# A clear, four selections and twelve subtractions put elsewhere in a gated cross-attention kernel with routed experts

## The chip, the cores and the metric

The kernel runs on one core of a Trainium2 chip. A core has five engines with queues of their own: TensorE (PE, with its weight loads shown as PEld), VectorE (DVE), ScalarE (ACT), GpSimd (POOL) and SyncE (SP). Each works through its instructions in order, and they meet through semaphores. TensorE writes its products to PSUM, which has eight banks of 128 x 512 float32 here; VectorE and ScalarE read them out, GpSimd works on SBUF alone. The metric is the device time of one execution in microseconds (us), lower is better.

## The reference

Four sequences of 512 tokens with 256 features pass through two layers. Each layer adds a gated cross-attention to a context of 512 tokens (16 heads of 16 features) and a gated feed-forward block. Reduced to what matters:

```python
x = x + tanh(g_xattn[0]) * L0_xattn(layernorm(x), ctx)   # with a bias by distance in time
x = x + tanh(g_ffn[0])   * L0_ffn(layernorm(x))          # weights rounded to -1, 0, 1; 256 -> 1024 -> 256
x = x + tanh(g_xattn[1]) * L1_xattn(layernorm(x), ctx)
x = x + tanh(g_ffn[1])   * L1_ffn(layernorm(x))

def L1_xattn(q, k, v):                                   # queries, keys and values after a relu
    E = NORM * einsum('bqhd,bkhd->bhqk', qh, kh)
    return einsum('bhqk,bkhd->bqhd', softmax(E, axis=-1), vh)

def L1_ffn(x):                                           # 2048 tokens, 4 experts, the best one of each token
    expert = argmax(x @ W_router, axis=-1)
    h = gelu(einsum('th,ehi->tei', x, W1) + b1, approximate=False)
    y = einsum('te,tei->ti', one_hot(expert, 4), h) @ Wo + bo + x
    return layer_norm(y) * ln_gamma + ln_beta
```

## The kernel before

**Attention.** Work is cut into 32 groups (layer, sequence, half of the heads' tiles, even or odd heads), in that order, and each group into four units, 128 in all. Per unit, `scores` (L535) issues two kinds of products: those whose rows give each query's maximum (`maxima`, L500; VectorE reduces them, L512), six units ahead, and those that give the weights (`weights`, L516; ScalarE takes the exponential, L527; in layer 0 GpSimd multiplies a block by the decay, L530). The maximum is subtracted ahead of time, inside the query: after the last maxima of a group, `shifted` (L563) turns them with four TensorE transposes into one PSUM bank (pmT) and VectorE subtracts this bank from the queries (L571). `slot` (L1199) places that call in the third unit of the group before, so the next group's first weights stand two units later. `weighted` (L548) multiplies with the values, `divided` (L600) turns the sums and divides, and in layer 1 adds them to x (L623, GpSimd mostly).

All other work (projections, layer norms, the first feed-forward block, routing) is a list of steps with a cost and a due unit, and `slot` puts them between units in program order. So every engine's order is fixed when the program is built.

**Routing.** `route` (L709) normalizes a sequence, writes rows to DRAM, and ranks each token within its expert. `dispatch` (L781) makes lists of tokens per tile of 128, four lists in all. For list i: `lists` and `token_places` (many small VectorE operations), `by_tile` (L950: a one-hot of tile and token, `tid`, in a cleared space of 128 x 512), `picked` (L983: four selections `sel` of 128 x 512 at L986 for 16 token blocks), `collected` (L994: TensorE products `pidT` of tid and sel, read out by ScalarE), `tokens` (L1006: the token numbers, which later row fetches need). The fourth list (i = 3) is of three mixed tiles, each of two experts.

**Experts.** After the attention 16 tiles (TT) go through `turn_tile` (t: transposes ptx, L1065), `hidden_half` (h: products pg, L1090, and ScalarE's Gelu, L1116; tiles from 13 on have two experts and 64 products) and `output_tile` (o: products pyf, L1285). `sum_tile` (L1293), `norm_tile` (L1308) and `put_tile` (L1321) follow each o on VectorE, with a root on GpSimd (L1304) and an indirect store from GpSimd's queue. `fetch_rows` (L1030) and `fetch_weights` (L1047) are indirect DMAs from that queue too. The queue of items is written by hand (L1359); around the change it is t9, o8, t10, h9, h10, t11, o9, h11. What `dispatch` does in this part hangs on the items in the table `steps` (L1351), and each item's steps stand after its products and fetches and before its sums and norm:

```python
        ("h", 8): [mixes[2]], ("o", 7): [mixed_places], ("o", 8): [mixed_tiles],
        ("h", 9): mixed_sels, ("h", 10): [mixed_collected], ("o", 9): [mixed_tokens],
...
        if kind == "o":
            sum_tile(j)
        if kind == "o" and 0 < j < TT - 2:
            norm_tile(j - 1)
```

Here `mixed_tiles` is the fourth list's `by_tile`, `mixed_sels` its four `picked`. So VectorE has at o8: by_tile of the fourth list, sums of tile 8, norm of tile 7; then, at h9, the four selections. GpSimd has at o8: rows and weights of tile 12, the clear of tid (L959), the root of tile 8, the store of tile 6.

Of the kernel before, what the change touches and what calls it, by code (L numbers as in the profile page):

```python
# [11 lines left out]
F32 = mybir.dt.float32  # L12
U32 = mybir.dt.uint32
AF = mybir.ActivationFunctionType
ALU = mybir.AluOpType
# [4 lines left out]
P = 128  # L20
B, S, D = 4, 512, 256
# [30 lines left out]
def flamingo_kernel(ctx: ExitStack, tc: tile.TileContext, t: dict, out: bass.AP):  # L52
    nc = tc.nc
# [4 lines left out]
    const = ctx.enter_context(tc.tile_pool(name="const", bufs=1))  # L58
# [5 lines left out]
    def bank_psum(name):  # L64
        return ps.tile([P, 512], F32, tag="bank", name=name)
# [37 lines left out]
    wo0 = const.tile([P, NC, D], F32, tag="wo0", name="wo0")  # L103
# [288 lines left out]
    xTs, qs, ks, q2s, pos, os_ = {}, {}, {}, {}, {}, {}  # L392
# [170 lines left out]
    def shifted(s):  # L563

        g = groups[s]
        m = m_sb[g[0]][g[3]]
        pm = bank_psum(f"pmT{s}")
        for n in range(NT):
            nc.tensor.transpose(pm[:, ts(n, P)], m[:, n].rearrange("p h w -> p (h w)"), ident)
        q2s[g] = act.tile([P, S], F32, tag="q2", name=f"q2_{s}")  # L570
        nc.vector.tensor_tensor(q2s[g], qs[g], pm, ALU.subtract)  # L571

# [206 lines left out]
    def dispatch(i):  # L781
# [3 lines left out]
        behind = i > 1  # L785
# [3 lines left out]
        def small(shape, tag):  # L789
            return sml.tile([P, *shape], F32, tag=f"d_{tag}", name=f"{tag}_{nm}", bufs=1)  # L790

        def across(v, *shape):
            return v.to_broadcast([P, *shape])
# [4 lines left out]
        def space(name):  # L798
            if i == 1:

                if not spaces:
                    two = act.tile([P, 2, S], F32, tag="xT", name=f"{name}_{nm}", bufs=2)
                    spaces.extend(two[:, k] for k in (1, 0))
                return spaces.pop()
            if behind:
                return act.tile([P, S], F32, tag="sel", name=f"{name}_{nm}", bufs=5)
            return wts.tile([P, S], F32, tag="xg", name=f"{name}_{nm}", bufs=4)
# [142 lines left out]
        def by_tile():  # L950

            place1 = st["place1"]
            ge = small([TT, T_LIST + 1], "ge")[:, 0:K, 0 : T + 1]
            nc.vector.tensor_tensor(
                ge, across(place1.unsqueeze(2), K, T + 1),
                across(made["tiles_of"][:, 0 : T + 1].unsqueeze(1), K, T + 1), ALU.is_gt,
            )
            tid = space("tid").rearrange("p (k w) -> p k w", w=HP)
            nc.gpsimd.memset(tid, 0.0)  # L959
            st["tid"] = tid  # L960
            tid = tid[:, 0:K, 0:T]
            nc.vector.tensor_tensor(tid, ge[:, :, 0:T], ge[:, :, 1 : T + 1], ALU.subtract)
            nc.vector.tensor_tensor(tid, tid, across(made["token"][:, 0:K].unsqueeze(2), K, T), ALU.mult)
            row1 = small([TT], "row1")[:, 0:K]
            nc.vector.tensor_reduce(row1, ge[:, :, 1 : T + 1], AX.X, ALU.add)
            nc.vector.scalar_tensor_tensor(row1, row1, float(-P), place1, ALU.mult, ALU.add)
            st.update(row1=row1)
# [48 lines left out]
        if j0 == T_ONE:  # L1016
            return (
                [fewest_and_most(m) for m in range(T_MIX)], mixed_places, by_tile,
                [picked(k) for k in range(0, K, 4)], collected, tokens,
            )  # L1020
        return [
            (lists, 0, 0), (token_places, 0, 0), (by_tile, 0, 1),
            *((picked(k), 0, int(k == 0)) for k in range(0, K, 4)),
            (by_expert, 0, 0), (collected, 0.15 * LISTS[i][0] + 0.3, 1), (tokens, 0.3, 1),
# [174 lines left out]
    def slot(u):  # L1199
# [4 lines left out]
        if u % NT == 2 and u > 0:  # L1204
            s = u // NT
            if s + 1 < len(groups):
                shifted(s + 1)
                used += 0.5
            if s > 0 and not by_blocks(s - 1):
                divided(s - 1)  # L1210
                used += 0.5
# [38 lines left out]
    for u in range(-NT, n_units):  # L1250
        if u == 0:
            shifted(0)
            early_values()
            other_constants()
        if u == 4:
            maxima_places(1)
        if u == first_unit(0, B - 1) + 1:
            attn_w.append(load_attn(1))
        if u == first_unit(1, 2) + 2:

            wo1 = [const.tile([P, NF // 2, D], F32, tag=f"cT{i}", name=f"wo1{i}") for i in range(2)]
            for i, w in enumerate(wo1):
                rw = t["wo1"][i * FF // 2 : (i + 1) * FF // 2, :]
                nc.sync.dma_start(out=w, in_=rw.rearrange("(c p) f -> p c f", p=P))
        vs = [u + NT] if u < 0 else [2 * u + NT, 2 * u + NT + 1] if u < LEAD - NT else [u + LEAD]
        scores(u, [v for v in vs if v < n_units])
        if u < -NT + 2:
            values[u + NT][0]()
        if u == -NT + 1:
            early_rows()  # L1270
        if u == -1:
            keys[0](halves=[1])
        if u in totals:
            job, i = totals[u]
            job(i)
        slot(u)
# [55 lines left out]
    for f2 in range(2):  # L1332
# [15 lines left out]
    mixes, mixed_places, mixed_tiles, mixed_sels, mixed_collected, mixed_tokens = dispatch(3)  # L1348
# [3 lines left out]
        ("o", 1): [turn3], ("o", 2): [products3], ("o", 3): [logits3],  # L1352
        ("h", 5): [ranks3, lists, token_places, by_tile], ("o", 4): [*sels, by_expert],
        ("o", 5): [collected], ("h", 7): [tokens, mixes[0]], ("o", 6): [mixes[1]],
        ("h", 8): [mixes[2]], ("o", 7): [mixed_places], ("o", 8): [mixed_tiles],
        ("h", 9): mixed_sels, ("h", 10): [mixed_collected], ("o", 9): [mixed_tokens],
    }
    first = LISTS[2][1]
    queue = [("h", 4), ("o", 0), ("o", 1), ("o", 2), ("t", 5), ("o", 3), ("h", 5)]  # L1359
# [130 lines left out]
```

## Time and profile before

| | |
|---|---|
| time, median of 3 runs | 844.43 us (844.37 to 845.02) |
| time of the profiled execution | 841.69 us |
| its span | 839.6 us |
| TensorE busy | 809.5 us, 96% |
| VectorE busy | 568.7 us, 68% |
| ScalarE busy | 422.1 us, 50% |
| GpSimd busy | 270.3 us, 32% |

The times of the profile are those of one execution, and stand against its own 841.69 us. The page has 40 slices of 21 us each; a digit is the busy share of a slice in tenths, and PEclk is the clock that TensorE was granted. A line of the groups names the source line, the engine, what is written and read, the count, busy time and mean duration, and then the idle time just before, with what ended it. A line of the timeline has start and duration in us. In the chain of waits each line is what ended last, in order of time: start, duration, what. A busy TensorE is not TensorE at its peak: where the banks come free late, its products start apart from each other.

The groups of instructions that the change touches or that stand nearest to it:

```profile
L530 POOL TENSOR_TENSOR p<-p,dec 128x256 f32<-128x256 f32 x128 | 93.6, 735 | 177.1 <-ACT p L527 177.1
L561 ACT COPY oT<-po 128x512 f32<-128x512 f32 x32 | 18.7, 584 | 77.1 <-PE po L555 77.1
L571 DVE TENSOR_TENSOR q<-q,pmT 128x512 f32<-128x512 f32 x32 | 21.7, 677 | 1.1 <-PE pmT L569 1.1
```

### The profile page before, as it was taken

Reading aid. Unit: us, or ns where it says so; the run is one execution under the profiler, and the core shown is the slowest. Engines: PE = TensorE matmul, PEld = TensorE weight load, DVE = VectorE, ACT = ScalarE, POOL = GpSimd, SP = SyncE. Lnnn points to the kernel's source line nnn. Section 1 sums busy time; section 2 is a strip of 40 time slices with the busy share of each in tenths; the row PEclk is TensorE's granted clock in tenths of the full one; section 3 lists DMA queues with packets and bytes.
Section 4 is the critical chain, followed back from the end, with each engine's and each line's share of the span. In section 5 each row is a group of like instructions: output and inputs, shape, how many; then the busy total and the mean of one; then the engine's idle time right before and its main releaser. Section 6 shows DMA issues by size and latency. Waiting matters only on the chain. (4 is left out here: it accounts for less than half of the span.)

```text
span 839.6 us, 13573 instructions
## 1 busy us (share of the span) xinstructions
PE 809.5 (96%) x5220; PEld 452.3 (54%) x5220; DVE 568.7 (68%) x1272; ACT 422.1 (50%) x884; POOL 270.3 (32%) x439
## 2 busy tenths in 40 slices
PE   6999999999999999999999999999999999997995
PEld 3444344535464345544474444554445546896994
DVE  6868868766857676567746777448688663886443
ACT  2575555653645453455526475336655667332341
POOL 5636445524233253321101030002103422544522
PEclk9999999999999999999999999999999999998998
DMA  9200000000001000000000000000104331736620
GB/s 313 72 1 1 1 1 1 1 1 1 1 1 39 1 1 1 1 27 1 1 1 26 1 24 28 1 1 1 52 1 152 126 106 59 284 119 218 241 78 31
DMA packets 17712, 42.27 MB, mean 50 GB/s; under 512 B 2033, under 2 KB 12017, under 8 KB 15217
## 3 DMA queue, kind: packets, MB, share of 16 engines
q0 software_dynamic: 5104, 27.34, 9.3%
q1 hardware_dynamic: 12128, 13.54, 4.8%
q8 instruction: 41, 0.67, 0.3%
q10 hardware_dynamic: 416, 0.54, 0.2%
q14 instruction: 23, 0.18, 0.1%
HBM read 35.13 MB, written 6.29 MB: 49 GB/s over the span
## 5 line engine op out<-in xcount | busy, mean ns | idle before, releaser
L512 DVE TENSOR_REDUCE m<-pm 128x1 f32<-128x512 f32 x512 | 316.8, 682 | 107.2 <-PE psc L498 104.8
L527 ACT ACTIVATE p<-psc 128x512 f32<-128x512 f32 x512 | 267.1, 602 | 151.4 <-PE psc L498 148.9
L498 PE MATMUL psc<-q,k 32*128 32x512 f32 x1024 | 278.3, 622 | 0.2 <-DVE h L676 0.2
L498 PE MATMUL pm<-k,q 32*128 32x512 f32 x1024 | 262.2, 615 | 1.5 <-ACT q L485 0.9
L530 POOL TENSOR_TENSOR p<-p,dec 128x256 f32<-128x256 f32 x128 | 93.6, 735 | 177.1 <-ACT p L527 177.1
L498 PEld LDWEIGHTS pm<-k,q 32*128 32x128 f32 x1024 | 92.7, 184 | 83.8 <-issue 49.8
L498 PEld LDWEIGHTS psc<-q,k 32*128 32x128 f32 x1024 | 106.2, 183 | 51.6 <-issue 25.5
L555 PE MATMUL po<-p,v 128*32 128x512 f32 x1024 | 116.5, 595 | 1.9 <-DVE m L512 1.9
L555 PEld LDWEIGHTS po<-p,v 128*32 128x32 f32 x1024 | 31.7, 109 | 81.8 <-issue 60.8
L1090 PE MATMUL pg<-xs,wg 128*128 128x128 f32 x608 | 71.6, 276 | 0.4 <-DVE m L512 0.4
L1090 PEld LDWEIGHTS pg<-xs,wg 128*128 128x128 f32 x608 | 69.8, 192 | 3.8 <-DVE m L512 1.4
L623 POOL TENSOR_TENSOR x<-x,o 128x256 f32<-128x256 f32 x14 | 10.2, 728 | 174.4 <-DVE o L616 131.7
L1116 ACT ACTIVATE ha<-pg,wg 128x128 f32<-128x128 f32 x120 | 34.2, 368 | 53.6 <-PE pg L1090 53.6
L668 PE MATMUL ph<-xTf,w1q 128*128 128x512 f32 x128 | 60.0, 605 | 0.0
L1285 PE MATMUL pyf<-wo,ha 128*128 128x256 f32 x256 | 58.6, 384 | 0.0
L561 ACT COPY oT<-po 128x512 f32<-128x512 f32 x32 | 18.7, 584 | 77.1 <-PE po L555 77.1
L383 PE MATMUL py_f<-w2q,h 128*128 128x256 f32 x256 | 57.2, 381 | 0.0
L383 PEld LDWEIGHTS py_f<-w2q,h 128*128 128x128 f32 x256 | 48.0, 190 | 9.4 <-DVE m L512 3.0
L1285 PEld LDWEIGHTS pyf<-wo,ha 128*128 128x128 f32 x256 | 48.4, 194 | 6.2
L455 PE MATMUL pk<-cT,wk 128*128 128x512 f32 x68 | 35.3, 644 | 7.2 <-DMA cT<-in_ctxT_dram 7.2
L668 PEld LDWEIGHTS ph<-xTf,w1q 128*128 128x128 f32 x128 | 22.6, 189 | 30.4 <-issue 18.2
L388 DVE SCALAR_TENSOR_TENSOR x<-py_f,tg,x 128x512 f32<-128x512 f32 x8 | 6.0, 751 | 42.8 <-PE py_f L383 42.8
(256 smaller groups left out, 814.6 us busy)
## 6 DMA issues: line engine op xcount, KB each, us to landing
x<-in_x_dram SPq DMA_DIRECT2D x4, 512.0 KB, 8.8
rows_d<-xn_f SPq DMA_DIRECT2D x4, 512.0 KB, 3.0
rows_d<-x SPq DMA_DIRECT2D x4, 512.0 KB, 3.6
cT<-in_ctxT_dram SPq DMA_DIRECT2D x3, 512.0 KB, 9.6
w1q<-in_w_dram SPq DMA_DIRECT2D x1, 1024.0 KB, 8.9
w2q<-in_w_dram SPq DMA_DIRECT2D x1, 1024.0 KB, 11.2
wo<-in_wo_dram SPq DMA_DIRECT2D x2, 512.0 KB, 3.8
rows<-in_rows_dram SPq DMA_DIRECT2D x1, 640.0 KB, 9.1
```

The lines of the kernel that those rows point to most:

```text
L383: nc.tensor.matmul(py[:, n, :], lhsT=operand(c, n0 + n), rhs=w[:, c, :], start=(c == 0), stop=(c == chunks - 1),)
L455: nc.tensor.matmul(pp, lhsT=attn_w[layer][w][:, c, ts(tt, P)], rhs=src[:, c, :], start=(c == 0), stop=(c == NC - 1),)
L498: nc.tensor.matmul(out_, lhsT=lhs[r, ts(n, P)], rhs=rhs[r, :], start=True, stop=True)
L512: nc.vector.tensor_reduce(m[:, n, 2 * pair + i, r : r + 1], pm[i], AX.X, ALU.max)
L527: nc.scalar.activation(p[:, i, :], psc[i], AF.Exp, scale=SCALE)
L530: nc.gpsimd.tensor_tensor(d, d, dec.unsqueeze(1).to_broadcast([P, 2, P]), ALU.mult)
L555: nc.tensor.matmul(po[i * HP : (i + 1) * HP, :], lhsT=v_sb[b % 2][0][:, kt, c0 : c0 + HP], rhs=ps_exp[NT * s + kt, i // 2][:, i % 2, :], s ...
L561: nc.scalar.copy(pos[s], po)
L668: nc.tensor.matmul(ph, lhsT=w1q[:, c, ts(f, P)], rhs=st["xT"][:, c, :], start=(c == 0), stop=(c == NC - 1),)
L1090: nc.tensor.matmul(ph[:, f, :], lhsT=w[:, c, ts(f2 * NF // 2 + f, P)], rhs=xs[j][:, c, :], start=(c == 0), stop=(c == NC - 1),)
L1116: nc.scalar.activation(ha[:, f, :], (ha if src is None else src)[:, f, :], AF.Gelu, bias=biases[j][:, fa : fa + 1],)
L1285: nc.tensor.matmul(py, lhsT=hs[j, f // 4][:, f % 4, :], rhs=wo1[f // 4][:, f % 4, :], start=(f == 0), stop=(f == NF - 1),)
```

## The change

Three edits. In `shifted`, for the second layer's sequences 1 to 3 (twelve groups), ScalarE copies the bank of turned maxima into SBUF, in the place that the first layer's output weights had, and GpSimd subtracts it from the queries; the other twenty groups stay with VectorE. In `by_tile`, the clear of `tid` is VectorE's for the two lists made after the attention (`behind`), and GpSimd's for the others as before. In `steps`, the fourth list's selections move from h9 to o8, behind its `by_tile` and in front of tile 8's sums and tile 7's norm. The order of TensorE's instructions stays as it was.

```diff
@@ def shifted(s)
         q2s[g] = act.tile([P, S], F32, tag="q2", name=f"q2_{s}")
-        nc.vector.tensor_tensor(q2s[g], qs[g], pm, ALU.subtract)
+        if g[0] == 1 and g[1] > 0:
+
+            turned = const.tile([P, S], F32, tag="wo0", name=f"mT{s}")
+            nc.scalar.copy(turned, pm)
+            nc.gpsimd.tensor_tensor(q2s[g], qs[g], turned, ALU.subtract)
+        else:
+            nc.vector.tensor_tensor(q2s[g], qs[g], pm, ALU.subtract)
@@ def by_tile()
             tid = space("tid").rearrange("p (k w) -> p k w", w=HP)
-            nc.gpsimd.memset(tid, 0.0)
+            (nc.vector if behind else nc.gpsimd).memset(tid, 0.0)
@@ steps
-        ("h", 8): [mixes[2]], ("o", 7): [mixed_places], ("o", 8): [mixed_tiles],
-        ("h", 9): mixed_sels, ("h", 10): [mixed_collected], ("o", 9): [mixed_tokens],
+        ("h", 8): [mixes[2]], ("o", 7): [mixed_places], ("o", 8): [mixed_tiles, *mixed_sels],
+        ("h", 10): [mixed_collected], ("o", 9): [mixed_tokens],
```

## The prediction

> **What bounds the kernel now.** I read the page first: TensorE is busy in nearly every slice, so time can come back only where its row breaks.
>
> ```profile
> PE   6999999999999999999999999999999999997995
> PEclk9999999999999999999999999999999999998998
> ```
>
> Slice 37 (755 to 776 us) is the break, and the granted clock falls there too. The busy time by stretches says how much is lost:
>
> ```profile
> 740.00:760.00 20.00, 20.00 (x155) 18.14 (x154) 17.82 (x97) 5.46 (x19) 11.53 (x12) 1.00 0.51 176
> 760.00:780.00 20.00, 15.57 (x125) 13.17 (x124) 9.65 (x33) 5.57 (x19) 8.48 (x10) 0.83 0.66 227
> ```
>
> TensorE (first number after the comma) is full until 760, then idles 4.43 us of 20 at a clock of 0.83. The chain of waits goes straight through this hole:
>
> ```profile
> 760.07 3.59 PE pg L1090 x32
> 763.65 0.36 issue
> 764.01 1.03 POOL xr L1037
> 765.34 0.99 POOL wg L1053
> 766.33 0.55 POOL tid_d L959
> 766.90 0.22 DVE tid_d L962
> ...
> 767.60 0.43 DVE y L1296
> ...
> 770.35 0.54 DVE y L1317
> 770.89 0.61 DVE sel_d L986
> 771.50 0.14 issue
> 771.64 2.37 PE pidT_d L999 x32
> 774.00 0.62 PE ptx L1065 x2
> 774.62 4.44 PE pyf L1285 x16
> ```
>
> Read it from the end. TensorE's collecting products of the fourth list (pidT) wait for VectorE's first selection; that stands behind tile 8's sums and tile 7's norm; those stand behind tid, which GpSimd must clear first; and the clear is queued behind two DMA issues. VectorE's timeline has the same wait as one number, with its last work before it:
>
> ```profile
> 763.02 0.21 DVE L954 TENSOR_TENSOR ge_d<-place_d,tiles_of 128x64 f32<-128x64 f32 x1
> 766.90 0.21 DVE L962 TENSOR_TENSOR tid_d<-ge_d 128x48 f32<-128x48 f32 x1 [3.67 <-POOL tid_d L959]
> ```
>
> In layer 1 there is little to win: the stretch from 420 to 500 us has TensorE busy 79.80 of 80, that from 500 to 580 has 78.83 of 80.
>
> **Part 1, the clear and the selections (lists behind the attention).** TensorE, by its own timeline, ends the hidden products of tiles 9 and 10 at about 767.07 (64 products from 759.90 on) and would be ready for pidT then. VectorE after the change, from the rows above: ge ends at 763.23; the clear of 128x512 follows on VectorE itself. No such row exists there: its clear of 128x4 takes 0.06, GpSimd's of the same tile 0.54, VectorE's 128x512 operations some 0.6 each (2.48 for four selections). Bounds 0.3 and 0.7; I take 0.6, nearest to an operation of that width. Then the four small operations up to L966, 766.90 to 767.60, so 0.70; then four selections, 2.48. Sum: 763.23 + 0.6 + 0.7 + 2.5 = 767.0. So all four are there when TensorE asks, and it needs the first only then, the last 0.75 us later: a slack of some 0.7 us. At the upper bound nothing is lost.
>
> What TensorE then saves: pidT takes 1.01 at full clock (list 3's, at 740.58), the next ptx 0.22 and pyf 3.46 (at 745.47 and 745.69). 767.07 + 1.01 + 0.22 + 3.46 = 771.76, against 774.62 + 4.44 = 779.06: **7.3 us less**, of which 4.6 are the idle time, 1.4 the slow pidT (it was paced by the selections as they came) and 1.4 the two slow groups behind it. [...]
>
> What is moved with it. Tile 8's sums, formerly 767.60 to 769.71, start behind the selections at 767.0: they are earlier, not later, since the wait was longer than the selections. GpSimd loses the clear (0.54), so its reciprocal root, the store of tile 6 and the weights for tiles 13 and 14 (issued at 771.80 and 773.29) come some 0.6 earlier only, while TensorE is 7.3 earlier. Landing took 5.85 and 7.41 there, so 777 and 780; tile 13's products, at 793.67 before, want them at 786.4. The rows of tile 13 are fetched once its tokens are known (issued 779.85, landed 783.17): the tokens come at 772.4, the issue stands behind the weights of 14, at 774, and the rows land after them, at about 781; the transpose that wants them moves from 789.99 to 782.7. That is the narrowest margin, 1.7 us. Later fetches wait for buffers that TensorE frees, and move along.
>
> For the third list the clear changes sides too: there VectorE waited 0.52 for it (735.42), now it works 0.6; pidT at 740.51 comes 1.7 us after its last selection (738.77). Worth 0 to -0.1, hidden.
>
> **Part 2, the twelve subtractions of layer 1 (batches 1 to 3).** VectorE gives up twelve of the 32 operations of L571 (677 ns each): 8.1 us of an engine that is 68% busy. ScalarE takes twelve copies like L561's (128x512 from PSUM, 584 ns): 7.0 us. GpSimd takes twelve two-input 128x512 operations; between the rows L530 (128x256, 735 ns) and L656 (128x1024, 2.36 us) that is 1.27 us each by the line through both; the ends are bounds. So the queries come 0.6 + 1.3 = 1.9 us after the maxima's transposes and ScalarE's exponentials, instead of 0.7 after VectorE's maxima.
>
> Cover: the transpose is issued at the end of a unit, the queries are wanted a whole unit later. Group by group from the timelines: in the tightest the transposes end at 568.7 and ScalarE's exponentials at 569.26, so the copy ends at 569.85 and the subtraction at 571.1, and the first product with these queries starts at 573.12 (1.4 us spare if that unit itself comes 0.6 earlier); the next tightest have 2.6 (at 682) and 3.1 (at 607). GpSimd's queue holds no wait in front of any of them that would outlast this; behind it stand the additions to x (L623), formerly idle for 2 to 26 us before, and the small copy of biases. The copies on ScalarE fall into its idle time (1.7 us before L467 at 588.60, for instance). So the new way costs TensorE nothing, if 1.27 is near.
>
> Gain: VectorE works without a pause in a few places where TensorE waits for its banks: at 569 (waits of 0.47 and 0.52 on L512), at 630, 518 and 608 (score products of a unit take 3.17, 3.23 and 2.90 us from first to next, against 1.93 undisturbed). There 0.6 less on VectorE can pass through: 4 x 0.6 = 2.4 at most. [...]
>
> ```profile
> 520.08 0.51 DVE L758 TENSOR_TENSOR onehot<-onehot,order 128x16 f32<-128x16 f32 x1
> ...
> 683.86 0.79 DVE L820 TENSOR_TENSOR more_d<-left_d,tiles_of 128x64 f32<-128x64 f32 x1
> ```
> ```profile
> 519.84 0.73 POOL L623 TENSOR_TENSOR x<-x,o 128x256 f32<-128x256 f32 x1 [15.95 <-DVE top L755]
> ...
> 683.85 0.72 POOL L623 TENSOR_TENSOR x<-x,o 128x256 f32<-128x256 f32 x1 [10.76 <-DVE left_d L816]
> ```
>
> L757 beside it, same size, takes 0.17, and L820 alone 0.23 (731.48); under GpSimd's addition they last until it ends. The new subtraction is 1.27 instead of 0.73 and is followed by the same addition. VectorE's two-SBUF-input operations behind a shift are L758 (at 518 and 608), an addition L623 (at 645) and the third dispatch (at 683); the maxima read PSUM and are free. [...] I take **1.0 us gained**, between 4 gained and 3 lost.
>
> **Sum.** 7.3 + 1.0 = 8.3 us. The profiled execution took 841.69 with a span of 839.6; it becomes 833.4. The shown runs stand at a median of 844.43, 2.7 above the profiled one; the hole is not a matter of which run, so I take the same 8.3 off: **836.1**.
>
> **Rivals.**
> [...]
> 2. *VectorE's relief passes through more fully*: scores in layer 1 are stretched by more than 10 us in all beyond 1.93 per unit, and a bank freed by ScalarE early (some 628.6 instead of 630.98) helps more than the operation itself. 7.3 + 4 gives about 833.
> 3. *Slower: the queries become the wait.* One mechanism: TensorE's second unit after each shift waits for GpSimd. By the spare times (1.4, 2.6, 3.1, 3.2, 3.3, 3.9, others 5 and more) a subtraction of 2.36 costs nothing; one of 5.8 (4.5 later) costs 1.9 + 3.1 + 1.4 + 1.3 + 1.2 + 0.6 = 9.5, which eats the tail's 7.3 and the rest: about 847 with nothing gained from VectorE. From about 5.3 on it decides. [...]
> 4. *It does not do what it says*: the selections still come late, because the wait before tid was for something other than the clear. Then about 844. Against: the clear ends at 766.87, tid starts at 766.90.
>
> **How the numbers follow.** Forecast (835 to 837.8) 0.50; rival 1 0.23; rival 2 0.19; rival 4 0.04; rival 3 0.04. A measurement here tells some 0.2% (1.7 us) from no change. Faster: the first three, 0.92; same 0.04; slower 0.04. The range takes the forecast with most of both neighbours: 832.5 to 840.5.
>
> **What would show it.** pidT of the fourth list starts within 0.3 us of the end of tile 10's products and takes about 1.0; the granted clock from 755 to 775 is 1.00; VectorE's clear lasts 0.3 to 0.7; the transpose of tile 13 has no wait on a DMA. In layer 1: GpSimd's subtraction at 1.2 to 1.4 us, no TensorE wait on it; L758 and L820 longer than before. I am wrong if TensorE has a new gap of over 1 us behind pidT, or if the score products after shifts lengthen.

## The result, and the profile after

The changed kernel takes **835.38 us** (median of 4 runs, 835.25 to 835.46), the kernel before beside it 844.40 (843.14 to 845.02): a ratio of 0.9894, with a 95% interval of 0.9882 to 0.9907, or 9.0 us less. The profiled execution took 835.46 with a span of 833.8.

The rows of the page by slices, PE and its granted clock, with the break in slice 37 gone:

```profile
PE   5999999999999999999999999999999999999995
PEclk9999999999999999999999999999999999999998
```

The busy time by stretches (first TensorE, then weight loads, VectorE, ScalarE, GpSimd; the third number from the end is the granted clock) says the same of the stretch that lost 4.43 us at a clock of 0.83:

```profile
740.00:760.00 20.00, 20.00 (x155) 18.13 (x154) 17.73 (x95) 5.37 (x19) 11.41 (x12) 1.00 0.46 165
760.00:780.00 20.00, 20.00 (x171) 18.70 (x170) 14.38 (x49) 8.01 (x28) 11.85 (x12) 1.00 0.65 221
```

The chain of waits no longer leaves TensorE here. Before, it went over GpSimd's clear, VectorE's sums and norm and the first selection:

```profile
761.22 7.15 PE pg L1096 x64
768.37 1.01 PE pidT_d L1005 x32
769.38 0.37 PE ptx L1071 x2
769.75 3.46 PE pyf L1291 x16
773.20 0.11 PE pid_d L1014
773.31 3.57 PE pg L1096 x32
```

The 64 hidden products of tiles 9 and 10 run into the collecting products pidT, which take 1.01 instead of 2.37 us. VectorE's timeline shows why nothing waits:

```profile
764.51 0.21 DVE L960 TENSOR_TENSOR ge_d<-place_d,tiles_of 128x64 f32<-128x64 f32 x1
764.78 0.48 DVE L965 MEMSET tid_d<- 128x512 f32 x1
765.30 0.21 DVE L968 TENSOR_TENSOR tid_d<-ge_d 128x48 f32<-128x48 f32 x1
...
766.11 2.50 DVE L992 TENSOR_TENSOR sel_d<-from_one,row_d 128x512 f32<-128x512 f32 x4
768.52 0.42 DVE L1302 TENSOR_TENSOR y<-xr,rows 128x256 f32<-128x256 f32 x1
```

The clear stands directly behind `ge`, and none of these lines has a bracket for an idle time: the wait of 3.67 us for GpSimd is gone. The selections start 2.26 us before pidT, the last ends at 768.61, 0.24 after pidT has begun and before its turn comes; tile 8's sums follow behind them.

In layer 1, the groups of the page that answer to L571 before (line, operation, count, busy and mean ns, then idle time in front of it):

```profile
L575 POOL TENSOR_TENSOR q<-q,mT 128x512 f32<-128x512 f32 x12 | 15.3, 1275 | 132.9 <-ACT mT L574 132.9
L577 DVE TENSOR_TENSOR q<-q,pmT 128x512 f32<-128x512 f32 x20 | 13.5, 676 | 0.0
```

Twelve subtractions went from 677 ns on VectorE to 1275 ns on GpSimd, and GpSimd's idle time in front of them holds up nobody: the list of waits has no TensorE wait on a `q` of GpSimd's.

### The profile page after: what moved, and what is told of

It is laid out like the page before. It is cut to its first block, busy times and chain, and to the rows that moved or that the text cites. A ratio compares the mean times of both kernels' runs of the same rounds, so it can differ in the third digit from the quotient of the medians.

```text
span 833.8 us, 13593 instructions
## 1 busy us (share of the span) xinstructions
PE 808.3 (97%) x5220; PEld 452.1 (54%) x5220; DVE 567.4 (68%) x1262; ACT 428.1 (51%) x896; POOL 285.1 (34%) x449
## 5 line engine op out<-in xcount | busy, mean ns | idle before, releaser
L512 DVE TENSOR_REDUCE m<-pm 128x1 f32<-128x512 f32 x512 | 317.0, 682 | 110.3 <-PE psc L498 107.3
L575 POOL TENSOR_TENSOR q<-q,mT 128x512 f32<-128x512 f32 x12 | 15.3, 1275 | 132.9 <-ACT mT L574 132.9
```

The source lines that it names most:

```text
L512: nc.vector.tensor_reduce(m[:, n, 2 * pair + i, r : r + 1], pm[i], AX.X, ALU.max)
```

## The experiments

Groups are numbered 0 to 31 in the order of the work; the twelve that the change moves are 20 to 31. A comparison of two profiles by their spans alone misleads by up to 3 us here (see E1), so each profile is also cut at TensorE's own marks: the transposes of a group's maxima (pmT), the third and fourth lists' pidT, and the pid behind the fourth. These stretches, in us, are the differences of TensorE's start times in each trace:

```
stretch                      before again  shifts only  tail only  clear only  order only  changed
group 19's pmT to 27's             182.20       181.11     182.20      182.20      182.21   181.10
group 27's pmT to 28's              20.77        20.30      20.77       20.77       20.77    20.30
group 28's pmT to 30's              37.49        37.15      37.44       37.50       37.46    37.15
group 31's pmT to list 3's pidT     59.03        58.76      59.03       59.03       59.03    58.76
list 3's pidT to list 4's pid       37.91        39.29      31.37       34.09       33.82    31.37
that pid to the last pyf            43.38        43.38      43.38       43.38       43.45    43.38
```

### E1: before, again

> The kernel before, once more, for a second profile of it: its profiled execution took 841.69 us where its other runs lie at 843.1 to 845.0, while the changed kernel's four runs lie within 0.2 us of 835.4. Theory A (the first profile was a lucky one at the start or in the attention, and the hole in front of the fourth list's products is always the same): time 844 us, the hole again 4.4 us of idle time with pidT at 2.4 us, and the extra 2 to 3 us stand before 700 us. Theory B (the hole itself varies, with the phase of TensorE's clock): pidT and the products behind it are slower than in the first profile by 2 to 3 us, and the part before 700 us is as it was.

844.03 us, ratio 0.9999 (0.9990 to 1.0008). Its profile differs from the first one of before in two places that no edit touches. TensorE's second group of transposes starts at 44.2 to 44.7 us in seven of the fourteen profiles and at 45.4 to 45.9 in the other seven, which are the ones whose clock was at half for 3.41 us from 27 to 29 us on. And a unit between the transposes ptx at about 641 and group 29's pmT takes 2.9 us in the first profile of before, but 4.2 to 4.3 in this one, in the four below and in that of the changed kernel: ScalarE's third exponential waits 1.8 us there. The first profile of before has the early start and the short unit, which can account for its 841.69 lying 2.7 below the median. The hole itself is the same 4.42 us. Its clock is not:

```profile
760.00:780.00 20.00, 15.49 (x123) 13.15 (x122) 10.56 (x37) 5.47 (x19) 8.33 (x9) 0.91 0.64 231
```

0.91 here against 0.83, so the clock's part of the hole varies between executions (the last section says how).

### E2 and E3: the two parts alone

E2 takes the clear and the order, and leaves the shifts with VectorE:

```diff
-            nc.gpsimd.memset(tid, 0.0)
+            (nc.vector if behind else nc.gpsimd).memset(tid, 0.0)
...
-        ("h", 8): [mixes[2]], ("o", 7): [mixed_places], ("o", 8): [mixed_tiles],
-        ("h", 9): mixed_sels, ("h", 10): [mixed_collected], ("o", 9): [mixed_tokens],
+        ("h", 8): [mixes[2]], ("o", 7): [mixed_places], ("o", 8): [mixed_tiles, *mixed_sels],
+        ("h", 10): [mixed_collected], ("o", 9): [mixed_tokens],
```

> The clear on VectorE and the early selections alone, the twelve subtractions left with VectorE. My theory: the tail is worth 7.0 us and the rest 1 to 2, so 844.4 - 7.0 = 837.4 us, and pidT of the fourth list starts as soon as tile 10's products end. Rival (the subtractions are worth nothing or cost): 835.4 us or less. Second rival (the subtractions bring half of it): 840 us.

E3 takes the shifts, and leaves the clear and the order as they were:

```diff
-        nc.vector.tensor_tensor(q2s[g], qs[g], pm, ALU.subtract)
+        if g[0] == 1 and g[1] > 0:
+            turned = const.tile([P, S], F32, tag="wo0", name=f"mT{s}")
+            nc.scalar.copy(turned, pm)
+            nc.gpsimd.tensor_tensor(q2s[g], qs[g], turned, ALU.subtract)
+        else:
+            nc.vector.tensor_tensor(q2s[g], qs[g], pm, ALU.subtract)
```

> The twelve subtractions on ScalarE and GpSimd alone; clear and selections as before. [...] Rival (no gain, TensorE was the bound there): 844.4 us. Second rival (the queries come late at GpSimd): above 845 us, with TensorE waits on L575.

E2: 837.83, ratio 0.9933 (0.9909 to 0.9956), 5.7 us less by the ratio and 6.5 by the medians. E3: 841.89, ratio 0.9974 (0.9966 to 0.9983), 2.2 to 2.5 less. The two are near the whole 9.0 together, and the table says that they do not meet: E2 changes only the stretch in front of the fourth list's pid (37.91 to 31.37), E3 only the four stretches above it (2.2 in all, of which the 0.34 between groups 28 and 30 is less than the 0.53 by which the changed kernel and E11, the same program, differ there). The changed kernel has both to the hundredth. E3's own tail of 39.29 is the hole at its more expensive clock (0.83).

How a subtraction less on VectorE reaches TensorE shows behind group 25, in E2 (VectorE subtracts) and then in the changed kernel:

```profile
570.76 0.68 DVE L571 TENSOR_TENSOR q<-q,pmT 128x512 f32<-128x512 f32 x1
571.36 0.25 DVE L609 RECIPROCAL rec<-pn 128x16 f32<-128x16 f32 x1
...
573.33 2.45 DVE L512 TENSOR_REDUCE m<-pm 128x1 f32<-128x512 f32 x4
574.04 1.13 PE L498 MATMUL pm<-k,q 32*128 32x512 f32 x4 [0.47 <-DVE m L512]
```
```profile
570.39 0.25 DVE L615 RECIPROCAL rec<-pn 128x16 f32<-128x16 f32 x1
...
572.36 2.45 DVE L512 TENSOR_REDUCE m<-pm 128x1 f32<-128x512 f32 x4
573.08 1.13 PE L498 MATMUL pm<-k,q 32*128 32x512 f32 x4 [0.47 <-DVE m L512]
```

TensorE waits for VectorE's first reduction in both, and the reduction starts 0.97 us earlier, of which 0.44 had been gained before.

### E4 and E5: the clear alone, the order alone

E4 is the first hunk of E2's diff, E5 the second.

> Only the clear goes to VectorE; the selections stay at h9, behind tile 8's sums and tile 7's norm. My theory, from the first profile's rows: ge ends at 763.2, clear 0.5, four small operations 0.7, sums and norm 3.2, first selection 0.6: pidT starts at 768.4 instead of 771.6, an idle time of 1.3 us that is too short for the clock to fall, and is paced by the selections to about 770.5; so 4.8 us gained, 839.6 us. Rival (the clear alone closed the hole, the selections' place is worth nothing): 837.4 us. Second rival (the clock falls all the same): 841 us.

> The selections alone move, in front of tile 8's sums; the clear stays with GpSimd. My theory: VectorE still waits for the clear until 766.9, then 0.7 for four small operations and 0.6 for the first selection, so pidT starts at 768.4 and is paced to about 770.3 without a slow clock: 844.4 - 4.8 = 839.6 us, near the clear alone (measured 840.2), so that either half alone gives most of what both give and the two do not add up. Rival (the place of the selections does all the work): 837.8 us. Second rival (it does nothing without the clear): 844.4 us.

E4: 840.22, ratio 0.9951 (0.9935 to 0.9968). E5: 839.74, ratio 0.9949 (0.9932 to 0.9967). Each alone brings some 4.2 us, both 6.5: they are not a sum, since both shorten one and the same wait. E4's chain of waits:

```profile
766.41 0.49 DVE tid_d L959
766.93 0.22 DVE tid_d L962
...
767.62 0.43 DVE y L1296
...
770.37 0.55 DVE y L1317
770.92 2.42 DVE sel_d L986 x4
773.38 0.43 PE pidT_d L999 x8
```

With the clear on VectorE the selections still stand behind the sums and the norm, and TensorE waits 1.59 us in front of pidT. In E5 the order is the new one, and the clear is what is late, as VectorE's timeline shows:

```profile
768.66 0.21 DVE L962 TENSOR_TENSOR tid_d<-ge_d 128x48 f32<-128x48 f32 x1 [3.68 <-POOL tid_d L959]
...
769.47 2.50 DVE L986 TENSOR_TENSOR sel_d<-from_one,row_d 128x512 f32<-128x512 f32 x4
```

VectorE's wait of 3.68 us is whole, and TensorE's hole is 1.32. Both have a pidT that is paced by the selections (the pieces from pidT to pid last 5.80 in place of 4.74), and neither has lost clock, here E4:

```profile
760.00:780.00 20.00, 17.98 (x152) 15.99 (x151) 14.25 (x52) 5.92 (x21) 9.90 (x11) 1.00 0.76 267
```

So the 6.5 us of the table are a hole of 4.42, 1.06 of pacing (5.80 less 4.74) and 1.0 of clock (E1's 6.79 from pidT to pid, less 5.80). Either edit alone shortens the hole by about 3 and frees the clock whole; what only the two together bring is the last 1.3 to 1.6 of the hole and the pacing.

### E6, E9 and E10: how late may the queries come

The changed kernel with n more passes of GpSimd over the copied maxima before each subtraction; n is 3 in E6, 1 in E9 and 2 in E10:

```diff
             nc.scalar.copy(turned, pm)
+            for _ in range(n):
+                nc.gpsimd.tensor_scalar(turned, turned, 0.0, None, ALU.add)
             nc.gpsimd.tensor_tensor(q2s[g], qs[g], turned, ALU.subtract)
```

> The changed kernel, with three more passes of GpSimd over the copied maxima (in place, adding zero) in front of each of the twelve subtractions; at 1.56 us each, as the row of a 128x512 GpSimd operation in the first profile, the queries come 4.7 us later. My theory: what is lost is what exceeds the spare time of each group in the changed kernel's profile (1.5 us in the tightest, then 2.7, 2.7, 2.8, 3.3, 4.2, others 5 and more): 3.2 + 2.0 + 2.0 + 1.9 + 1.4 + 0.5 = 11.0 us, so 846.4 us, slower than the kernel before. Rival (TensorE never waits for these queries): 835.4 us. Second rival (each group loses the whole delay): 891 us.

> The changed kernel with one more pass of GpSimd over the copied maxima (adding 0) in front of each of the twelve subtractions: 1.49 us more each, as the three passes took before. Theory (only the spare time counts): group 25 has 1.51 us spare, all others over 2.6, so nothing waits and the time is that of the changed kernel, 0.989 of before, within 0.002; no TensorE wait on the queries of over 0.2 us. Rival (the longer use of SBUF by GpSimd holds VectorE and so TensorE's banks): 1 to 3 us more, 0.991 to 0.993, with longer score products after the shifts and no wait on the queries.

> As the run before with two more passes, 2.98 us more each. By the spare times 1.51, 2.69, 2.72, 2.78 TensorE waits 1.5, 0.3, 0.3 and 0.2 us for the queries, 2.3 in all. Theory (a short wait in the scores also costs a spell of half clock, 3.4 us each time, as with three passes): at least group 25 gets it, 2.3 + 3.4 = 5.7 above the changed kernel, 0.996 of before; at two or three places 0.1 us of waiting would already do it, 9 to 12.5 above, 1.000 to 1.004. Rival (the clock fell with three passes only because the waits were longer than 0.8): 2.3 above, 0.992, granted clock 1.00 throughout.

E9: ratio 0.9877 (0.9859 to 0.9895). E10: 0.9905 (0.9876 to 0.9935). E6: 851.8 us, **1.0085** (1.0057 to 1.0113), slower than before and slower than the 846.4 expected. One pass takes 1.49 us, as E6's group by form shows (shortest, median, longest in ns):

```profile
L576 POOL TENSOR_SCALAR mT<-mT x36: 1487/1489/1516, 457.0 to 701.7; 128x512 f32<-128x512 f32 x36
```

TensorE's waits on these queries (us in total, times, longest) are, in E6 and then in E10; E9 has none on them:

```profile
PE psc L498 <- POOL q L577: 7.5, 5, 2.8
```
```profile
PE psc L498 <- POOL q L577: 1.7, 2, 1.2
```

So 1.5 us more cost no wait, 3.0 cost 1.7 in all, and 4.5 make the kernel slower than before. E10's 1.7 us against some 2.3 reckoned from the spare times, and E6's 7.5 against 9.6, say that the spare times are a fair measure, a little on the safe side. But E6 lost 17.1 us in the stretches against the changed kernel, not 7.5. The rest is clock. The stretches around its wait at group 25, cut where the granted clock changes:

```profile
573.24:576.65 3.41, 0.60 (x6) 0.28 (x8) 3.11 (x8) 0.00 (x0) 3.24 (x4) 1.00 0.00 0
576.65:580.06 3.41, 3.41 (x16) 0.95 (x16) 0.12 (x1) 1.12 (x3) 2.80 (x9) 0.50 0.02 5
580.06:583.48 3.42, 3.42 (x20) 0.79 (x16) 2.19 (x6) 1.05 (x2) 0.00 (x0) 0.50 0.00 0
583.48:586.89 3.41, 3.41 (x34) 1.14 (x24) 0.54 (x1) 1.55 (x4) 0.00 (x0) 1.00 0.00 0
```

TensorE is busy again from 576.37, yet at half clock from 576.65 to 583.48. The missing clock (half of 6.83 us) is 3.4 us. The same happens behind the waits of groups 27 and 28 (620 to 628, 644 to 652), 3.4 each again: 10.2 in all, which with 7.5 makes 17.7 for the 17.1 lost.

E10's rival in its expectation, that its shorter waits cost no clock, is the one that held in the profiled execution (832.79 us):

```profile
560.00:580.00 20.00, 18.29 (x140) 7.81 (x136) 13.98 (x32) 10.62 (x21) 7.37 (x12) 1.00 0.00 1
```

Whether it held in all is open: another of E10's four executions took 837.52 us at a mean granted clock of 0.991, against 0.996 in the profiled one. A spell of half clock would fit that; no trace of it was kept.

### E7 and E8: which of the twelve bring something

E7 leaves groups 23, 27, 29 and 31 with VectorE, those behind which VectorE has operations with two inputs from SBUF; E8 moves only 23, 25, 27 and 28, where TensorE waited for VectorE's banks:

```diff
-        if g[0] == 1 and g[1] > 0:
+        if g[0] == 1 and g[1] > 0 and s not in (23, 27, 29, 31):
...
-        if g[0] == 1 and g[1] > 0:
+        if s in (23, 25, 27, 28):
```

> The changed kernel with groups 23, 27, 29 and 31 back on VectorE: those behind whose shift VectorE has operations with two SBUF inputs, which GpSimd's subtraction can hold up. By the changed kernel's profile these four gain 0.46, 0.48, 0.34 and 0.27 us all the same. My theory now: 835.4 + 1.5 = 836.9 us. [...]

> The changed kernel with groups 23, 25, 27 and 28 alone on ScalarE and GpSimd, the four in whose stretches TensorE waited for VectorE; the other eight back on VectorE. My theory: 835.4 + 0.3 + 0.3 (groups 29 and 31) = 836.0 us. Rival (relief adds up over all twelve, as VectorE is behind everywhere): 2/3 of the gain of 2.5 us lost, 837.1 us.

E7: ratio 0.9894 (0.9875 to 0.9914). E8: 0.9887 (0.9868 to 0.9906). Neither can be told from the changed kernel by its time; the marks tell them apart. Against the kernel of E2, TensorE of the changed kernel comes earlier by 0.44 at 524 (behind group 23), 0.53 more at 577 (25), 0.47 more at 614 (27) and 0.60 more at 634 (28), of which some 0.3 are given back by 652, behind group 29. E8 has the four first ones alike (0.40, 0.53, 0.47, 0.60); E7 only the second and the fourth (0.53 and 0.54). So the four places carry nearly all, the other groups next to nothing, and leaving the four groups out forgoes 0.8 us at TensorE's marks (E7 against the changed kernel at 616). What it saves is the 0.3 behind group 29: from that group's pmT to group 30's the changed kernel and E3 take 18.95, and E2, E7 and E8, which leave group 29 with VectorE, 18.71, all five with the long unit of 4.2 us or more in front. The 0.27 in front of the third list's pidT is there in E7 and E8 too, though neither moves group 31; its cause stays open.

### E11 and E12: the changed kernel and E9, side by side

E9 had the lowest ratio so far, and a short unit at 641 (2.9 us from ptx to pmT). E11 is the changed kernel once more, E12 is E9 once more.

> The changed kernel itself once more, beside the one with one extra GpSimd pass. Its first profile had a unit of scores and weights before 645.6 that took 4.1 us where the kernel with one and with two extra passes, and the first profile of before, took 2.5. Theory (that unit falls one way or the other from execution to execution, in whatever kernel): 0.988 to 0.990 of before, the two kernels within 0.001 of each other. Rival (the later subtraction is what shortens that unit): the changed kernel 0.989, long unit, and the one with the extra pass 1.5 us faster.

> One extra GpSimd pass in front of each subtraction, again, on the chip of the run before. Theory: the same time as the changed kernel beside it, within 0.8 us. Rival: 1.5 us faster than it, 0.987 to 0.988 of before, with the short unit (2.5 us from its transposes ptx to pmT, not 4.1).

E11: 834.64, ratio 0.9888 (0.9871 to 0.9904). E12: 833.24, ratio 0.9873 (0.9856 to 0.9889). The intervals overlap, so a gain by the later subtraction is not shown, though the medians are 1.4 apart. The short unit is not E9's: it takes 3.2 in E11, where the first profile had 4.3, and 3.7 in E12, where E9 had 2.9. Only 0.5 us between group 19's and 27's transposes (180.63 in E9 and E12, 181.10 and 181.11 in the changed kernel) comes back in both profiles. What decides the unit was not found. No version among these is shown to be faster than the changed kernel.

## Why the prediction was right, step by step

**The hole in front of pidT** (7.3 less). Right in mechanism and nearly in size. Against the same first profile of before the stretch from the third list's pidT to the fourth's pid went from 38.39 to 31.37, 7.0; against E1's it is 6.5, since the clock there cost less. The clear took 0.485 us (reckoned at 0.6, between 0.3 and 0.7), pidT 1.01 as said, at the end of tile 10's products, at a clock of 1.00. The idle time of 4.6 in the sum is too long by 0.15: the wait of 4.42 before 771.64 began at 767.22, not at 767.07. The ptx behind pidT took 0.37 in place of the 0.22 used. The margin between the last selection's end and its use was reckoned at 0.7; it ends at 768.61, and by the same reckoning is wanted at 768.37 + 0.75, so 0.5.

**A hole closed in part** (E4's 1.3 us, "too short for the clock to fall"). Right for the case: in E4 and E5 pidT waits 1.59 and 1.32 us, the granted clock stays at 1.00, and the clock's part is gained all the same. By the length alone it does not hold: E6 lost the clock behind waits of 1.31 and 0.87.

**What is moved with it** (rows of tile 13 with 1.7 us to spare). Nothing waited: their fetch was issued at 775.71, and the transposes at 784.13 started without a wait. The trace does not give the landing itself, so how much of the margin is left stays open.

**The way over ScalarE and GpSimd costs nothing if it is near 1.27 us.** Right: 1.275 for the subtraction and 0.592 for the copy (reckoned 0.584). The tightest groups have 1.5 (25), 2.7 (31, 27) and 2.8 (28) us to spare, against 1.4, 2.6 (31), 3.1 (27) and 3.2 or 3.3 reckoned.

**VectorE's relief** (2.4 at most, in four places). Right in its places, and 2.0 of the 2.4 came there: 0.53 and 0.60 behind groups 25 and 28, and 0.44 and 0.47 behind 23 and 27, where VectorE also meets GpSimd.

**The holds under GpSimd** (1.4 of the 2.4 lost again). This is the term that was mis-sized, and by which the gain in layer 1 was put at 1.0 and came out at 2.2. The loss of 1.4 in it was the author's estimate and no run shows it; E3's four stretches showed the gain of 2.2 in its place. On VectorE the holds are there. Timelines of the changed kernel, VectorE's and then GpSimd's:

```profile
647.79 0.92 DVE L629 TENSOR_TENSOR x<-x,o 128x256 f32<-128x256 f32 x1
...
684.94 1.16 DVE L822 SCALAR_TENSOR_TENSOR left_d<-count,taken 128x4 f32<-128x4 f32 x1
686.13 0.72 DVE L826 TENSOR_TENSOR more_d<-left_d,tiles_of 128x64 f32<-128x64 f32 x1
```
```profile
647.13 1.30 POOL L575 TENSOR_TENSOR q<-q,mT 128x512 f32<-128x512 f32 x1 [4.88 <-ACT mT L574]
...
684.81 1.27 POOL L575 TENSOR_TENSOR q<-q,mT 128x512 f32<-128x512 f32 x1 [10.29 <-ACT mT L574]
```

The addition took 0.42 before, and the operation at 684.94 took 0.15. Each started beside GpSimd's subtraction and ended only behind it: at 648.71 against 648.43, and at 686.10 against 686.08. The reductions of the maxima (L512), which read PSUM, were not held: all 512 took 657 to 693 ns, with GpSimd at work beside them or not. Set against before, VectorE's operations last longer by 0.50 and 0.94 us in these two places, in the second beside the old hold, which stayed (0.79 before, 0.72 now). At 521 and at 610 it is only 0.14 each, since there the new hold takes the place of most of the old one: the operation that the prediction names went from 0.51 to 0.37, and the one two places behind it from 0.17 to 0.45. These 1.7 us on VectorE are not far from the 1.4 that was taken off. What the estimate had wrong is that TensorE would lose them: TensorE's marks lack some 0.1 behind each of groups 23 and 27 and 0.24 behind 29, and nothing behind 31.

**Rival 3, late queries** ("from about 5.3 on it decides", 847 for 5.8). The mechanism is real and dearer than reckoned. E6's three passes and the subtraction take 3 x 1.49 + 1.26 = 5.73 us, and by its ratio of 1.0085 it stands 7 us above before, with VectorE's relief included, where 847 was put without it. The working counted waits only; the clock behind them cost more than the waits did.

**Rivals 2 and 4.** Nothing took the place of the hole (no new TensorE wait of over 0.2 us in the list of waits). Of the fuller relief there is about half: 2.2 lies between the forecast's 1.0 and rival 2's 4. The wait in front of tid was for the clear: it goes with the clear in E4, and stays with it in E5.

The sum is thus 6.5 to 7.0 + 2.2, or 8.7 to 9.2, against 8.3 said and 9.0 measured. The sum is nearer than its parts because the tail brought less than said and layer 1 more, and that is luck.

## What to carry to other kernels

When the chain of waits runs through several engines into one hole, add up each engine's remaining queue with the repair in it before choosing one: here a clear and an order were each late for the same hole, and either alone brought 4.2 us of the 6.5. Relief of a busy engine is worth something only where the bound engine waits for it just then; list these places with their size (four of twelve here), and take the other operations as free of gain. When an operation is given to a slower engine with time to spare, the waits beyond that spare time can bring on a loss of clock that is larger than they are: 10.2 us for 7.5 in the one kernel that went far beyond it, none for 1.7 in the profiled execution of the one that went a little.

## What was not expected of the hardware

The granted clock does not follow the length of a wait alone. In E6 a wait of 2.81 us, one of 1.31 and one of 0.87 were each followed by 6.83 us at half clock (3.4 us lost each), while waits of 2.01 in the same kernel (group 31), 1.59 (E4), 1.32 (E5) and 1.24 (E10) left the clock at 1.00. E10's stands in the same place as the first of those that cost.

Two things in the traces tell them apart. In each of the fourteen, all changes of the clock lie whole multiples of 3.41 us apart (in E6 at 576.65, 583.48, 621.02, 627.85, 644.92 and 651.74), and between two stretches of full clock it was at half for one or two such steps. The other is the work that TensorE does within one step. As a measure, take the columns of each product times its form as a share of the largest form in the traces, 128*128: a score product is 32*128 with 512 columns in TensorE's rows, so it counts 128. The products pg, 128*128, make 64 x 128 columns in 7.31 us, so some 3,820 in a step. Over all steps that began at full clock, the clock fell behind 27 (the kernel's end in all fourteen traces, the start in seven, the hole in three, and three in E6), and none of these has more than 1,579. It stayed full behind 3,296, of which one has 1,576 and all others 1,611 or more. E6's three steps have 273, 1,241 and 1,428. Its wait of 2.01 is cut by the end of a step and leaves 1,611, E10's wait of 1.24 leaves 1,620, and those of E4 and E5 leave 1,862 and 2,625.

So in these traces a short wait cost the clock sooner in front of score products, which count for a quarter of their columns (1.31 and 0.87 in E6), than in front of pidT and the 128*128 products behind it (1.59 and 1.32 in E4 and E5 cost nothing), and E10's was spared narrowly. Where the steps begin differs from execution to execution. This is read from the traces after the fact; no kernel was built to test it.

It also says why one and the same hole of 4.42 us was granted 0.83 over its 20 us in one execution and 0.91 in another: the clock was at half for two steps in the first profile (769.67 to 776.50) and for one in E1 (773.95 to 777.37). One such step of 3.41 us at half clock costs 1.7 us; each of E6's three waits, of 2.81, 1.31 and 0.87 us, all shorter than a step, cost two.
